# The last batch of a two-layer graph network: k pieces among its first steps, statistics a step later, one PSUM tile for each row block of the last projection

## The chip, the cores and the metric

The kernel runs on one core of a Trainium2 chip. The metric is the device time of one execution in microseconds; lower is better. The engines are named as the profile names them: PE (TensorE, matrix products into PSUM), DVE (VectorE), ACT (ScalarE), POOL (GpSimd, which works on SBUF only) and SP, whose queue issues most DMA transfers.

## The reference, cut to what matters

Two layers on x of shape 32 x 512 x 512 (batches, nodes, features), with one 512 x 512 graph `adj` for all batches.

```python
# layer 0
mi, mj = x @ Wi.T, x @ Wj.T
x = layernorm(x + deg * (mi + b) + adj @ mj)
# layer 1: masked attention, 8 heads of 64
q, k, v = split_heads(x @ Wq.T + bq), split_heads(x @ Wk.T + bk), split_heads(x @ Wv.T + bv)
attn = softmax(where(adj == 0, -inf, q k^T / 8))
x = layernorm(x + (attn v) @ Wo.T + bo)
```

All of it is float32. Each layer norm takes mean and variance over the 512 features of a row.

## The kernel before

**Pieces.** The 512 x 512 products with Wi, Wj, Wq, Wk, Wv and Wo are not done as 4 x 4 block products but by a seven-product scheme on 256 x 256 quarters. `piece(kind, b, i, bank)` issues one of the seven products (i from 1 to 7) of one projection (`l0` for layer 0, `q`, `k`, `v`, and `pj` for the output projection): four matrix instructions, or eight for `l0`, into a PSUM bank `mma` or `mmb`, then an evacuation on DVE (L445, L456, L465 or L472) or ACT (L434). Pieces of one group (X: 1, 2; Y: 6, 7, 4; Z: 5, 3) accumulate into the same bank, and each needs one weight tile, which SP loads ahead into a ring of seven. Combinations of quarters that the pieces need (`combos`, L396) are subtractions on POOL.

**Attention.** For a batch b there are eight steps: two groups g of four heads, four chunks kc of keys. A step does `scores` (L481, into two `sc` tiles of PSUM), exponentials in place on ACT (L485), a multiplication with the 0/1 graph on DVE (L486, result `e`, four buffers), and a step later `values` (L503) from e. `presum` adds up the e tiles of the chunks: the first two chunks on POOL (L492), later ones on DVE (L494). At the end of a group, `sums` (L513) makes the sums over keys on PE, `drain` (L518) copies them to SBUF on ACT, `invert` (L522) takes reciprocals in four parts on DVE, `scale` (L538) multiplies the values with them into `oT`, and `tell` (L526) adds up the reciprocals for a check that decides at the end of the program whether a slower general version must run.

**Order.** The order of instructions on each engine is the order in which the Python code issues them; there is no scheduler behind it. `PERIODS[n]` lists the work that is issued between the steps of batch n − 1's attention: layer 0 and the projections of the batch n, the output projection of the batch before last, the first parts of the batch after. `by_steps` spreads a period's list over its eight steps by cost (1.73 us a piece), with the halfway mark of the last ordinary period carried over to period 31. `phase_a(32)`, the end of period 31, holds five of the seven k pieces of the last batch, 31 (counted from 0). Period 32 is `last_steps`: beside the attention of batch 31 there are only the seven `pj` pieces of batch 30, its statistics (`stats`: L289, L290 on DVE, L291 to L293 on POOL), its scaling (`apply`, L296 on ACT), its `store`, and `last_part`. In each step the period's work comes after the scores and values; the `rest` of a finished group (inverts, scales, tell) and late presums are issued between the pieces, one after a piece, or in step 0 all of it at once after the first piece or `FLUSH`.

**The end.** `last_part` is batch 31's output projection without the seven-product scheme: per row block ic (four of 128 rows) an identity product that brings in the residual, and four products c with Wo, of which c = 2 and 3 need the oT of the second group of heads. `ACC[ic]` is the PSUM place of a row block: banks mma and mmb for blocks 0 and 1, and for blocks 2 and 3 the halves of one `sc` tile. `last_rows` takes a block's statistics, scales it on ACT and stores it. The final group of heads has no drain: `invert(1, ic, 0)` takes the reciprocals from the sums in PSUM, and `tell_all` makes both check sums on DVE (L533).

Of the kernel before, what the change touches and what calls it, by code (L numbers as in the profile page):

```python
# [14 lines left out]
OP = mybir.AluOpType  # L15
# [10 lines left out]
def gnn_attention_kernel(  # L26
# [36 lines left out]
    nc = tc.nc  # L63
    B, N, D = x.shape
# [15 lines left out]
    def work(shape, name, bufs, dtype=FT):  # L80
        return pools.work.tile(shape, dtype, name=name, bufs=bufs)
# [4 lines left out]
    def mm_tile(bank):  # L86
        return psum.tile([P, 512], FT, name="mm" + bank, bufs=1)
# [4 lines left out]
    def sc_tile():  # L92
        return psum.tile([P, 2, N], FT, name="sc", bufs=2)
# [36 lines left out]
    def load_w(t, src, eng):  # L130
        eng.dma_start(t, rows(src))
        return t
# [21 lines left out]
    for name, src in (("wv", wvT), ("wq", wqT)):  # L154
        t = load_w(work([P, NC, D], "v", 2), src, nc.sync)
# [31 lines left out]
    told = const.tile([P, B * 4 + 1], FT, name="told")  # L187
# [193 lines left out]
    def quarter(src, j, n):  # L381
        return src[:, 2 * j:2 * j + 2, Q * n:Q * n + Q]

    def ot_quarter(b):
        return lambda j, n: OT[b, j][:, :, Q * n:Q * n + Q]
# [89 lines left out]
    E, ES, PV, RL = {}, {}, {}, {}  # L475
# [30 lines left out]
    def sums(g, kcs=(1,), last=1):  # L506

        if g not in RL:
            RL[g] = (sc_tile()[:, 0, :], work([P, N], "rl", 1))
        for kc in kcs:  # L510
            for h in range(4):
                src = ES[h // 2] if kc == 1 else E[h // 2, kc]
                nc.tensor.matmul(RL[g][0][32 * h:32 * h + 32, :], ones[:, :32], src[:, h % 2, :], start=(kc == 1), stop=(kc == last))  # L513

    def drain(b, g):

        j = 2 * (b * 2 + g)
        nc.scalar.activation(RL[g][1], RL[g][0], AF.Identity, accum_out=told[:, j:j + 1])  # L518

    def invert(g, part, src=1):  # L520
        c = slice(part * P, (part + 1) * P)
        nc.vector.reciprocal(RL[g][1][:, c], RL[g][src][:, c])  # L522

    def tell(b, g):
        j = 2 * (b * 2 + g) + 1
        nc.vector.reduce_sum(told[:, j:j + 1], RL.pop(g)[1], axis=AX.X)  # L526

    def tell_all(b, g):

        pl, rl = RL.pop(g)  # L530
        j = 2 * (b * 2 + g)
        nc.gpsimd.memset(told[:, j + 1:j + 2], 0.0)
        nc.vector.tensor_tensor_reduce(pl, pl, rl, 1.0, 0.0, OP.add, OP.add, told[:, j:j + 1])  # L533

    def scale(b, g, r, c=slice(0, N)):
        if (b, g) not in OT:
            OT[b, g] = work([P, 2, N], "oT", 3)
        nc.vector.tensor_mul(OT[b, g][:, r, c], PV[g][r][:, c], RL[g][1][:, c])  # L538

    def rest(b, g):  # L540
        return [(invert, g, c) for c in range(4)] + [(scale, b, g, 0), (scale, b, g, 1), (tell, b, g)]
# [7 lines left out]
    FLUSH = (0.0, None)  # L549

    def z(f, *a):
        return (0.0, f, *a)

    def pc(kind, b, i, bank):
        return (2 * PC if kind == "l0" else PC, piece, kind, b, i, bank)

    ORDER = (1, 2, 6, 7, 4, 5, 3)

    LATE = (5, 3, 6, 7, 4)
    ALONE = ((1, "a"), (6, "b"), (2, "a"), (7, "b"), (5, "a"), (4, "b"), (3, "a"))  # L560

    def banks(n):

        return ("a", "b") if n % 2 == 0 else ("b", "a")

    def phase_a(n):

        A, K = banks(n)
        if n == B:
            return [pc("k", n - 1, i, bank) for i, bank in ((6, K), (5, A), (7, K), (3, A), (4, K))]  # L570
        xq, aq = lambda j, m: quarter(XD[n], j, m), lambda j, m: quarter(AX_T[n], j, m)
        g = [(GA, l0_gather, n, dc, A) for dc in range(DC)]
        k = [pc("k", n - 1, i, K) for i in LATE]
        res = []
        for i in range(DC):
            res += g[i:i + 1] + k[i:i + 1] + [z(l0_turn, n, i)]
            if i in (1, 2):
                res += [z(base, n, i - 1)]
            if n == 1 and i in (1, 3):
                res += [z(combine, "wo", nc.vector, i // 2)]  # L580
            if i == 1:
                res += [z(combos, TX, n, xq, (1,)), z(combos, TA, n, aq, (1,))]
        return res + [z(combos, TX, n, xq, (2,)), z(combos, TA, n, aq, (2,)),
                      z(combos, TX, n, xq, (3, 4)), z(combos, TA, n, aq, (3, 4)),
                      pc("l0", n, 1, A), k[4]]
# [111 lines left out]
    def last_steps():  # L697

        m = B - 2
        p = {i: pc("pj", m, i, bank) for i, bank in ALONE}  # L700
        c = [z(combos, TO, m, ot_quarter(m), (1, 2)), z(combos, TO, m, ot_quarter(m), (3, 4))]
        own = [(4 * GA, last_part, c, 0) for c in range(2)]
        return [[z(last_load), FLUSH, c[0], p[1], c[1]], [p[2], p[6]], [p[5], p[7], z(add_bo, B - 1, 0), z(add_bo, B - 1, 1)],
                [p[3], p[4], z(stats, m, 0), z(stats, m, 1)], [z(apply, m, 0), z(apply, m, 1), z(store, m)], [own[0]], [own[1]], []]

    def run(f):
        f[1](*f[2:])
# [2 lines left out]
    ACC = {}  # L710
# [5 lines left out]
    def last_part(c, half=None, ic=None):  # L716
        if c == 0:
            if half == 0:
                ACC[0], ACC[1] = mm_tile("a"), mm_tile("b")
            else:  # L720
                t = sc_tile()
                ACC[2], ACC[3] = t[:, 0, :], t[:, 1, :]
        for ic in (range(2 * half, 2 * half + 2) if ic is None else (ic,)):
            if c == 0:

                nc.tensor.matmul(ACC[ic], ident, XT[B - 1][:, ic, :], start=True, stop=False)
            nc.tensor.matmul(ACC[ic], OT[B - 1, c // 2][:, c % 2, ic * P:(ic + 1) * P], W["wo"][c // 2][:, c % 2, :],  # L727
                             start=False, stop=(c == 3))

    def last_rows(ic):  # L730
        y = XT[B - 1][:, ic, :]
        mv = work([P, 5], "mv", 12)
        ln_stats(mv, ACC[ic])
        nc.scalar.activation(y, ACC[ic], AF.Identity, bias=mv[:, 4:5], scale=mv[:, 3:4])
        nc.sync.dma_start(rows(out[B - 1])[:, ic, :], y)

    def flags():
# [5 lines left out]
        nc.vector.tensor_scalar(again, tot, -1.0, 1.0, op0=OP.mult, op1=OP.add)  # L743

    PERIODS = [first() + phase_c(0) + phase_a(1)]
    half = None
    for n in range(1, B):
        todo = phase_b(n) + phase_c(n) + phase_a(n + 1)
        if n < B - 1:
            half = sum(f[0] for f in todo) / 2  # L750

        PERIODS += [by_steps(todo, half)]
    PERIODS += [last_steps()]
    for f in PERIODS[0] + [f for p in PERIODS[1:] for todo in p for f in todo]:
        if f[1] is piece:
# [9 lines left out]
    for n in range(1, B + 1):  # L765
        b = n - 1
        extra = []
        for step in range(STEPS):
            g, kc = divmod(step, NC)
# [27 lines left out]
    sums(1, (1, 2), 3)  # L797
    values(B - 1, 1, 3)
    sums(1, (3,), 3)
    for c in range(2):  # L800
        last_part(c, 1)
    for ic in range(NC):
        c = slice(ic * P, (ic + 1) * P)
        invert(1, ic, 0)
        scale(B - 1, 1, 0, c)
        scale(B - 1, 1, 1, c)
        last_part(2, ic=ic)
        last_part(3, ic=ic)
        if ic > 0:
            last_rows(ic - 1)  # L810
    tell_all(B - 1, 1)
    last_rows(NC - 1)
    flags()
    fast.close()
    flag = nc.values_load(again[0:1, 0:1], min_val=0, max_val=1)
    with tc.If(flag > 0), tc.tile_pool(name="general", bufs=1) as pools.work:
# [26 lines left out]
        with tc.For_i(0, B, 1) as b:  # L843
            g = "general"
# [6 lines left out]
            for ic in range(NC):  # L851
                c = slice(ic * P, (ic + 1) * P)
# [10 lines left out]
            for ic in range(NC):  # L863
                c = slice(ic * P, (ic + 1) * P)
                nc.vector.tensor_copy(V[g][:, ic, :], product([(HT[g][:, dc, c], wv[:, dc, :]) for dc in range(DC)]))
            for hp in range(HP):
                c = slice(hp * P, (hp + 1) * P)
# [35 lines left out]
            for ic in range(NC):  # L903
                c = slice(ic * P, (ic + 1) * P)
# [45 lines left out]
```

## Time and profile before

| What | Value |
|---|---|
| median of 4 runs | 3703.95 us (3703.35 to 3707.35) |
| profiled execution | 3705.69 us |
| its span, first to last instruction | 3703.6 us |
| PE busy | 3667.4 us, 99% of the span |
| DVE, POOL, ACT busy | 65%, 52%, 28% |
| mean granted PE clock | 0.997 |
| PE busy in 3613 to 3656 us | 39.44 of 43 us |
| PE busy in 3656 to 3676 us | 17.30 of 20 us |
| PE busy in 3676 to 3704 us | 15.31 of 28 us |

The busy time of PE is the time in which a matrix instruction is under way. The last three rows are windows of the trace: the eight steps of the last batch's attention begin at 3615.58 us and its last sums at 3676.97 us; the last ACT instruction ends at 3697.50 us. The three windows show how much of PE's time is idle in the part of the program that the change touches.

### The profile page before, as it was taken

Reading aid. Unit: us, or ns where it says so; the run is one execution under the profiler, and the core shown is the slowest. Engines: PE = TensorE matmul, PEld = TensorE weight load, DVE = VectorE, ACT = ScalarE, POOL = GpSimd, SP = SyncE. Lnnn points to the kernel's source line nnn. Section 1 sums busy time; section 2 is a strip of 40 time slices with the busy share of each in tenths; the row PEclk is TensorE's granted clock in tenths of the full one; section 3 lists DMA queues with packets and bytes.
Section 4 is the critical chain, followed back from the end, with each engine's and each line's share of the span. In section 5 each row is a group of like instructions: output and inputs, shape, how many; then the busy total and the mean of one; then the engine's idle time right before and its main releaser. Section 6 shows DMA issues by size and latency. Waiting matters only on the chain.

```text
span 3703.6 us, 49651 instructions
## 1 busy us (share of the span) xinstructions
PE 3667.4 (99%) x18474; PEld 2512.4 (68%) x18474; DVE 2391.0 (65%) x3134; ACT 1028.7 (28%) x1482; POOL 1941.8 (52%) x1985
## 2 busy tenths in 40 slices
PE   8999999999999999999999999999999999999997
PEld 5666667666676767676767666666666676767663
DVE  4566666666666666666666666666666666666665
ACT  2222232323322222222232222232222322222322
POOL 3466445555455564455554555545555545555443
PEclk9999999999999999999999999999999999999999
DMA  8444555455554455554455544555544556455541
GB/s 252 121 125 136 150 153 160 120 142 140 156 159 137 131 136 150 157 152 127 136 144 156 160 134 132 138 148 160 149 131 133 148 151 163 126 136 140 151 137 47
DMA packets 797173, 530.02 MB, mean 143 GB/s; under 512 B 530432, under 2 KB 611840, under 8 KB 796928
## 3 DMA queue, kind: packets, MB, share of 16 engines
q1 hardware_dynamic: 780384, 494.78, 49.8%
q10 hardware_dynamic: 16320, 31.46, 2.3%
q8 instruction: 151, 2.47, 0.3%
q14 instruction: 94, 0.77, 0.1%
q0 software_dynamic: 224, 0.53, 0.0%
HBM read 453.25 MB, written 73.40 MB: 142 GB/s over the span
## 4 chain that ended last, share of the span: by engine, by line
PE 96%; DVE 1%; SPq 1%; POOL 1%; DMA 0%; issue 0%; ACT 0%; DVEq 0%; POOLq 0%; ACTq 0%
PE mma L427 31%; PE mmb L427 31%; PE sc L481 13%; PE ov L503 12%; PE mmb L325 3%; PE mma L325 3%; PE sc L513 2%; SPq L113 0%; DVE e L486 0%; DVE rl L522 0%; DMA wv<-e 0%; SPq L144 0%; DVE st L289 0%; DMA xa<-hd 0%; PE sc L727 0%
## 5 line engine op out<-in xcount | busy, mean ns | idle before, releaser
L485 ACT ACTIVATE sc<-sc 128x1024 f32<-128x1024 f32 x512 | 493.1, 1006 | 1550.4 <-PE sc L481 1544.1
L486 DVE TENSOR_TENSOR e<-sc,edge 128x1024 f32<-128x1024 f32 x512 | 602.1, 1217 | 205.2 <-ACT sc L485 173.3
L427 PE MATMUL mmb<-ring,big 128*128 128x256 f32 x3144 | 733.0, 382 | 0.0
L427 PE MATMUL mma<-ring,big 128*128 128x256 f32 x3112 | 724.4, 381 | 2.5 <-ACT p L434 1.4
L427 PEld LDWEIGHTS mmb<-ring,big 128*128 128x128 f32 x3144 | 593.0, 190 | 132.1 <-issue 27.6
L427 PEld LDWEIGHTS mma<-ring,big 128*128 128x128 f32 x3112 | 585.8, 190 | 133.3 <-issue 26.5
L396 POOL TENSOR_TENSOR big<-big 128x512 f32<-128x512 f32 x376 | 492.7, 1339 | 32.1 <-DVE big L373 10.9
L481 PE MATMUL sc<-q,k 64*128 64x512 f32 x2048 | 509.0, 615 | 0.0
L503 PE MATMUL ov<-e,v 128*32 128x512 f32 x4096 | 492.5, 598 | 4.9 <-DVE oT L538 4.9
L492 POOL TENSOR_TENSOR es<-e 128x1024 f32<-128x1024 f32 x128 | 301.1, 2365 | 352.3 <-DVE e L486 352.3
L427 PE MATMUL mma<-big,ring 128*128 128x256 f32 x1808 | 432.1, 382 | 3.2 <-DVE k L465 3.2
L427 PE MATMUL mmb<-big,ring 128*128 128x256 f32 x1776 | 422.8, 381 | 1.0 <-DVE v L456 1.0
L291 POOL TENSOR_SCALAR mv<-mv 128x1 f32<-128x1 f32 x256 | 50.0, 195 | 670.5 <-DVE mv L290 658.0
L427 PEld LDWEIGHTS mma<-big,ring 128*128 128x128 f32 x1808 | 341.5, 190 | 77.0 <-issue 26.0
L427 PEld LDWEIGHTS mmb<-big,ring 128*128 128x128 f32 x1776 | 334.3, 190 | 73.4 <-issue 26.0
L503 PEld LDWEIGHTS ov<-e,v 128*32 128x32 f32 x4096 | 106.9, 109 | 352.2 <-issue 320.8
L204 POOL TENSOR_TENSOR xlo<-xh,xhi 128x512 fp32r<-128x512 f32 x128 | 164.1, 1294 | 336.9 <-ACT xhi L203 336.8
L481 PEld LDWEIGHTS sc<-q,k 64*128 64x128 f32 x2048 | 176.0, 186 | 207.4 <-issue 205.1
L340 POOL TENSOR_TENSOR big<-big,deg_r 128x512 f32<-128x512 f32 x124 | 174.1, 1404 | 266.8 <-DVE big L339 266.8
L494 DVE TENSOR_TENSOR es<-es,e 128x1024 f32<-128x1024 f32 x250 | 304.3, 1218 | 0.0
L445 DVE TENSOR_TENSOR xh<-xh,mma 128x512 f32<-128x512 f32 x186 | 126.7, 681 | 266.3 <-PE mma L427 266.3
L445 DVE TENSOR_TENSOR xh<-xh,mmb 128x512 f32<-128x512 f32 x186 | 126.7, 681 | 263.2 <-PE mmb L427 263.2
(155 smaller groups left out, 3660.7 us busy)
## 6 DMA issues: line engine op xcount, KB each, us to landing
ring<-wo SPq DMA_DIRECT2D x217, 256.0 KB, 2.8
ring<-wq SPq DMA_DIRECT2D x160, 256.0 KB, 3.9
ring<-wv SPq DMA_DIRECT2D x160, 256.0 KB, 3.4
ring<-wk SPq DMA_DIRECT2D x160, 256.0 KB, 3.3
ring<-wi SPq DMA_DIRECT2D x155, 256.0 KB, 2.7
ring<-wj SPq DMA_DIRECT2D x155, 256.0 KB, 2.6
xh<-in_x_dram SPq DMA_DIRECT2D x32, 1024.0 KB, 5.5
xa<-in_x_dram SPq DMA_DIRECT2D x124, 256.0 KB, 4.0
```

The lines of the kernel that those rows point to most:

```text
L204: nc.gpsimd.tensor_sub(lo, xs, hi.bitcast(FT))
L325: nc.tensor.matmul(pm, parts[w][:, jc, :], adjR[:, jc, :], start=(w == 0 and jc == 0), stop=(w == 1 and jc == NC - 1))
L340: nc.gpsimd.tensor_tensor(XD[b][:, dc, :], XD[b][:, dc, :], deg_r, op=OP.mult)
L396: nc.gpsimd.tensor_tensor(dst, p, q, op=OP.subtract)
L427: nc.tensor.matmul(pm[:, c * Q:(c + 1) * Q], lhs, rhs, start=first, stop=(kc == 1 and n == len(terms) - 1), skip_group_check=True)
L445: nc.vector.tensor_tensor(d, d, pm, op=OP.add)
L481: nc.tensor.matmul(ps[:, s, :], KT[b, hp // 2][r, hp % 2, kc * P:(kc + 1) * P], QT[b, hp // 2][r, hp % 2, :], start=True, stop=True)
L485: nc.scalar.activation(ps, ps, AF.Exp, scale=QSCALE)
L486: nc.vector.tensor_tensor(e, ps, edge[:, kc:kc + 1, :].to_broadcast([P, 2, N]), op=OP.mult)
L492: nc.gpsimd.tensor_add(ES[i], E[i, 0], E[i, 1])
L494: nc.vector.tensor_add(ES[i], ES[i], E[i, kc])
L503: nc.tensor.matmul(PV[g][r][32 * h:32 * h + 32, :], V[b][:, kc, c0:c0 + 32], E[h // 2, kc][:, h % 2, :], start=(kc == 0), stop=(kc == NC - 1))
```

## The change

The first pieces of the list: two of batch 31's k pieces, 7 and 4, leave period 31 and go to the first step of period 32, around piece 1 of batch 30's output projection. The three that stay in period 31 come as 5, 6, 3 instead of 6, 5, 7, 3, 4. Piece 4 of batch 30's projection moves from step 3 to step 4, its statistics from step 3 to step 5, and its scaling and store from step 4 to step 6.

In the end, each of the row blocks 2 and 3 has an `sc` tile of its own. The final sums are drained by ACT like the others, reciprocals are taken from the copy, and `tell` and the drain's own sum replace `tell_all`. The early parts of row blocks 2 and 3 (identity, c = 0, c = 1) no longer come all before the late parts of block 0: block 2's come before block 0's late parts, block 3's before block 1's.

```diff
     if n == B:
-            return [pc("k", n - 1, i, bank) for i, bank in ((6, K), (5, A), (7, K), (3, A), (4, K))]
+            return [pc("k", n - 1, i, bank) for i, bank in ((5, A), (6, K), (3, A))]
...
     def last_steps():
         m = B - 2
-        p = {i: pc("pj", m, i, bank) for i, bank in ALONE}
+        A, K = banks(B)
+        p = {i: pc("pj", m, i, K if i in (6, 7, 4) else A) for i in ORDER}
         c = [z(combos, TO, m, ot_quarter(m), (1, 2)), z(combos, TO, m, ot_quarter(m), (3, 4))]
         own = [(4 * GA, last_part, c, 0) for c in range(2)]
-        return [[z(last_load), FLUSH, c[0], p[1], c[1]], [p[2], p[6]], [p[5], p[7], z(add_bo, B - 1, 0), z(add_bo, B - 1, 1)],
-                [p[3], p[4], z(stats, m, 0), z(stats, m, 1)], [z(apply, m, 0), z(apply, m, 1), z(store, m)], [own[0]], [own[1]], []]
+        k = [pc("k", B - 1, i, K) for i in (7, 4)]
+        return [[z(last_load), k[0], FLUSH, c[0], p[1], c[1], k[1]], [p[2], p[6]], [p[5], p[7], z(add_bo, B - 1, 0), z(add_bo, B - 1, 1)],
+                [p[3]], [p[4]], [own[0], z(stats, m, 0), z(stats, m, 1)], [own[1], z(apply, m, 0), z(apply, m, 1), z(store, m)], []]
...
     def last_part(c, half=None, ic=None):
         if c == 0:
             if half == 0:
                 ACC[0], ACC[1] = mm_tile("a"), mm_tile("b")
             else:
-                t = sc_tile()
-                ACC[2], ACC[3] = t[:, 0, :], t[:, 1, :]
+                ACC[ic] = sc_tile()[:, 0, :]
...
     sums(1, (3,), 3)
-    for c in range(2):
-        last_part(c, 1)
+    drain(B - 1, 1)
     for ic in range(NC):
         c = slice(ic * P, (ic + 1) * P)
-        invert(1, ic, 0)
+        invert(1, ic)
         scale(B - 1, 1, 0, c)
         scale(B - 1, 1, 1, c)
+        if ic < 2:
+            last_part(0, 1, ic + 2)
+            last_part(1, 1, ic + 2)
         last_part(2, ic=ic)
         last_part(3, ic=ic)
         if ic > 0:
             last_rows(ic - 1)
-    tell_all(B - 1, 1)
+    tell(B - 1, 1)
     last_rows(NC - 1)
```

The banks of the seven `pj` pieces stay the same (1, 2, 5, 3 in mma; 6, 7, 4 in mmb). `tell_all` and the argument `src` of `invert` are removed.

More of the change, by code (lines that the diff above doesn't have):

```diff
@@ L518, in drain, with invert @@
         nc.scalar.activation(RL[g][1], RL[g][0], AF.Identity, accum_out=told[:, j:j + 1])
-    def invert(g, part, src=1):
+    def invert(g, part):
         c = slice(part * P, (part + 1) * P)
-        nc.vector.reciprocal(RL[g][1][:, c], RL[g][src][:, c])
+        nc.vector.reciprocal(RL[g][1][:, c], RL[g][1][:, c])
     def tell(b, g):
@@ L526, in tell @@
         nc.vector.reduce_sum(told[:, j:j + 1], RL.pop(g)[1], axis=AX.X)
[L528 to L533, printed above, removed]
     def scale(b, g, r, c=slice(0, N)):
@@ L559, in gnn_attention_kernel @@
     LATE = (5, 3, 6, 7, 4)
-    ALONE = ((1, "a"), (6, "b"), (2, "a"), (7, "b"), (5, "a"), (4, "b"), (3, "a"))
     def banks(n):
```

## The prediction

> **What bounds the kernel now.** First the page, its chain of work that ended last:
>
> ```profile
> PE 96%; DVE 1%; SPq 1%; POOL 1%; DMA 0%; issue 0%; ACT 0%; DVEq 0%; POOLq 0%; ACTq 0%
> ```
>
> The kernel is TensorE (PE) work from end to end. The change keeps every matrix product, so it can only win or lose time in which PE waits, and in the stretch after the last sums, where PE is no longer the bound. So I read next the timeline from 3569 us on, for idle time ahead of PE's groups (in brackets: us, releaser):
>
> ```profile
> 3583.62 1.92 PE L503 MATMUL ov<-e,v 128*32 128x512 f32 x16 [0.64 <-DVE oT L538]
> ...
> 3602.78 1.99 PE L427 MATMUL mmb<-big,ring 128*128 128x256 f32 x8 [0.98 <-DVE v L456]
> ...
> 3625.30 1.92 PE L503 MATMUL ov<-e,v 128*32 128x512 f32 x16 [1.19 <-DVE oT L538]
> ...
> 3651.75 1.06 PE L513 MATMUL sc<-es,ones 128*32 128x512 f32 x8 [1.99 <-DVE e L486]
> ...
> 3658.70 1.92 PE L503 MATMUL ov<-e,v 128*32 128x512 f32 x16 [3.09 <-DVE oT L538]
> ...
> 3694.49 0.70 DVE L289 BATCH_NORM_STATS2 st<-sc 128x6 f32<-128x512 f32 x1 [1.47 <-ACT xh L734]
> ```
>
> Five PE waits of 7.9 us in all, and in the tail a statistic that waits for ScalarE (ACT). The chain of waits in order of time says what stands behind two of them:
>
> ```profile
> 3625.99 1.29 POOL big L396
> 3627.28 3.68 POOL xh L442 x3
> 3630.97 2.46 POOL big L396 x2
> 3633.42 4.63 POOL es L492 x2
> 3638.08 1.22 DVE e L486
> ...
> 3647.29 0.70 DVE st L289
> ...
> 3650.59 1.12 DVE e L486
> 3651.75 1.97 PE sc L513 x16
> ```
>
> From the last scaled oT of batch 30 the path runs through four kinds of POOL work to VectorE's (DVE's) e, which writes a buffer that the presum on POOL still reads; later the statistics (four L289/L290 pairs) stand ahead of e, and the sums on PE need that e to free their PSUM buffer.
>
> The profiled execution took 3705.69 us (span 3703.6, 2.09 around it), 1.74 above the median of 3703.95; the terms below are differences inside its span, and I subtract them from the median.
>
> **The change, part by part.** I lay the built order of the changed program's instructions over the durations of these rows: a piece 1.73 us (1.83 to 1.93 behind another tile shape), the scores of a step 1.92, its values 1.85, a sums group 0.86; sums to drain 1.10, drain to reciprocal 0.73, four reciprocals to the first oT 3.49, oT to values 0.74.
>
> *Two k pieces moved.* Batch 30's last four steps hold 3, 4, 4, 3 pieces instead of 4 each, and batch 31's first step three instead of one. Work on PE: nothing (−3.46 and +3.46); what counts is waits.
> - Step 5 of batch 30's period: the values wait for oT. Before, its last reciprocal stood behind a q evacuation that waited for the fourth piece; now it follows directly, so oT comes 1.15 us earlier (3581.73 for 3582.88), but PE arrives 1.73 earlier. The wait grows by 0.6.
> - The wait of 0.98 at 3602.78 (a bank whose evacuation stood late on DVE) goes. Before, two groups in bank mmb followed each other there, the second waiting for the first one's evacuation; now the first k piece there is 5, in mma, and the banks alternate. −1.0.
> - First step of batch 31: PE has 5.4 us of pieces instead of 1.9 between the sums and the scores. The oT chain is 1.8 us longer, because on DVE the evacuation of the first k piece (3.0 us after the sums start, 0.6 long) now stands ahead of the reciprocals. PE reaches the values at 8.25 us after the sums, oT is there at 7.9: the 1.19 goes, −1.2, with 0.4 to spare.
> - POOL's chain above starts 1.8 us later after the sums but PE's scores come 3.5 later, so the 0.26 that PE lost at step 3's scores (2.18 us for 1.92, 3638.23 to 3640.41) goes too: −0.25. What is late next: DVE's e of step 2 ends just as those scores need its buffer.
>
> *Pieces 3 and 4 of pj apart, statistics a step back.* Without the statistics ahead of e, step 4's sums find their buffer free: −2.0. But step 3 is one piece shorter, while DVE's run from e of step 2 to e of step 3 keeps its 5.64 us (3638.08 to 3643.72, with two L494 at 1.7 beside POOL's L378, where L494 else takes 1.22). Counted from the sums, e of step 3 frees its buffer at 27.5 and PE asks at 26.7: a new wait of 0.8 to 1.0, or none if the L494 run at 1.22. I take 0.9, as the rows beside L378 are the same rows.
> - Piece 4 now lies between step 4's sums and step 5's scores, in the wait of 3.09. It fills 1.7 us of it, but its evacuation stands on DVE ahead of the reciprocals and delays them by 1.7. Left: 3.0, −0.1.
> - Statistics in step 5: on POOL their twelve small operations (5.0 us, 3648.30 to 3653.32) now stand between the two presums L492. Queued behind: the second presum; who waits: the second e of step 6, which needs its buffer, then the scores of step 7, which need that e's PSUM. The second presum ends 10 us after the first starts; e comes 3.3 us late, step 7's scores 1.1. +1.1. Bounds: 0 (if POOL's operations ran with no gaps) to 3.3 (if nothing hid it).
> - apply and store of batch 30 move behind: 2.9 us of ACT between step 6's and step 7's exponentials, free there; the 1 MB store is issued some 24 us before the last row, and landed in 5.5 us or less in rows of its size. Nothing. The wo load's eight issues (3.7 us of SP) pass two ring loads that are used three steps later: nothing.
>
> *The tail, from the start of the last sums (3676.97).* Before, the last ACT starts 19.75 us later (3696.72). After: a drain on ACT comes between, so the first reciprocal is at 1.83 instead of 1.10. PE needs no oT until 0.97 + 0.96 + 2 x 0.86 = 3.65 (identity and two products of row block 2); oT is there at 3.3, so the 0.73 costs nothing. It costs up to 0.73 if oT came later than 3.65. Then two products for block 0 (end 5.37), three for block 3 (7.95), two for block 1 (9.67; block 1's end was at 9.7 before too), two for block 2 (11.4). DVE: statistics of block 1 at 9.87, reciprocal 10.7, oT 11.65, PE 11.99 to 14.0 for block 3; its statistics at 14.0, and from there 2.23 to the last ACT (3694.49 to 3696.72) is 16.25. Before, block 1's statistics stood behind block 2's scaling, 0.5 later; and as blocks 2 and 3 shared a tile, block 2's statistics waited for block 3's products (3691.45) and block 3's for block 2's ACT (3694.49), 3.0 more. −3.5. What follows (last DMA, end: 3697.50 to 3703.6) moves with it.
>
> Sum: +0.6 −1.0 −1.2 −0.25 −2.0 +0.9 −0.1 +1.1 −3.5 = −5.5 us, so 3698.5.
>
> PE's longest wait stays about 3 us, and the granted clock of these stretches is 1.00 up to 3694, through the 3.09; it falls to 0.50 only after the last products. The Trainium skill (TensorE: Matmul & The Clock Gate, Part 1: The HAM clock gate) says that an idle window of about 3.4 us halves the clock, and that the window runs freely. By that rule a wait of 3.0 stays just inside and the trace agrees so far; by it a wait stretched past 3.4 would cost what the fourth rival below says.
>
> **The rivals.**
> 1. The new waits are hidden: no wait for e in steps 4 and 7 and none added in batch 30's step 5. For: they hang on 0.3 to 1 us of DVE order and on the slow L494. Against: the rows of POOL's statistics are regular, 1.27 each. −5.5 −0.9 −1.1 −0.6 = −8.1: 3695.9.
> 2. Slower than before: POOL's run from oT to e of step 2 is the bound in batch 31's first steps, and now has no margin. If its 12.1 us (L396, L442, L492) stretch, each us is a us of PE. For: L378 ran at 1.73 beside L494, a plain row at 1.25, ratio 1.4. Against: in these rows it runs beside e and evacuations and keeps 1.25. At 1.4 it takes 4.9 more, 3703.4; above a ratio of 1.46 (5.6 us) the change is slower; at 1.6 it is 3705.8.
> 3. The middle gives nothing: waits only move on, and the tail alone counts. For: DVE is busy 31.3 of 43 us and takes each early PE back in the next step. −3.5 plus the step-5 and step-7 costs of 1.7: −1.8, 3702.1.
> 4. The clock: a wait of 3.0 grows past a window and halves the clock for a while. The windows view has lowered clocks of 0.85 and 0.54 between 54 and 60 us and of 0.67 and 0.71 between 105 and 116, so stretches of some 3.4 to 7 us. Cost half of that: 3700.2 to 3702.0. Against: 3.09 passed without it.
>
> **How the numbers follow.** A change of 0.2% is 7.4 us, about what a measurement of this kernel can tell from no change. Forecast: 0.56, between −7.5 and −3.4 by the bounds above (step 7 between 0 and 3.3, e between 0 and 1); a tenth of it lies past 7.4. Rival 1: 0.28, nearly all past 7.4. Rival 2: 0.06; slower by over 7.4 would need a ratio of 2.07, which is half of its chance at most. Rival 3: 0.06. Rival 4: 0.04. Faster by over 0.2%: 0.06 + 0.26 = 0.32; slower by over 0.2%: 0.03; within: 0.65. The range reaches from rival 1 with the tail 1 us better, 3694.9, almost to rival 3, 3701.5.
>
> **What would show it.** In the timeline after: no bracket at the values of batch 31's step 1 and at step 4's sums; about 3.0 ahead of step 5's values; a wait of 1 for e in step 7's scores, with a presum on POOL just before; 16.3 us from the last sums to the last ACT. Wrong if the tail keeps 19 us, if PE waits over 2 us for e in step 2 or 3 of batch 31 (rival 2), or if the granted clock is below 1.00 before the last products.

## The result, and the profile after

The changed kernel takes 3698.27 us (median; 3695.32 to 3701.78), the kernel before in the same comparison 3704.29 us (3700.61 to 3708.73). The ratio is 0.9983, 95% interval 0.9978 to 0.9987. The forecast was 3698.5 us. The profiled execution took 3699.72 us with a span of 3697.9.

All traces below are cut at the same five places: **A** from the scores of step 4 in batch 30's attention to batch 30's last sums, **B** from there to the values of batch 31's step 5, **C** to the last sums, **D** to the start of the last ACT instruction, **E** to the end of the span. A to D are differences of two start times in the timeline, E of the span and a start time. What lies ahead of A is not touched by any edit, but A begins anywhere between 3565.69 and 3569.94 us in the traces, and E wanders between 6.36 and 7.03; the time of a single execution carries both.

| us | A | B | C | D | E |
|---|---|---|---|---|---|
| before | 49.98 | 39.46 | 18.27 | 19.75 | 6.88 |
| after | 45.90 | 40.01 | 19.66 | 16.24 | 6.40 |
| difference | −4.08 | +0.55 | +1.39 | −3.51 | −0.48 |
| forecast | −3.86 | +0.81 | +1.1 | −3.5 | 0 |

(The forecast's row is its terms regrouped: two pieces of 1.73 leave A and enter B; beside them A holds +0.6 and −1.0, and B the terms from −1.2 to −0.1.) First the page's chain of work that ended last, after:

```profile
PE 96%; DVE 1%; SPq 1%; POOL 1%; DMA 0%; issue 0%; ACT 0%; POOLq 0%; DVEq 0%; ACTq 0%
```

The same as before: still TensorE from end to end. The timeline after, at the places that were shown of before, and two new ones (start, duration, engine, line, output and inputs; in brackets the idle time ahead and what ended it):

```profile
3582.95 1.92 PE L503 MATMUL ov<-e,v 128*32 128x512 f32 x16 [1.26 <-DVE oT L531]
...
3623.86 1.92 PE L503 MATMUL ov<-e,v 128*32 128x512 f32 x16
...
3643.04 2.26 PE L481 MATMUL sc<-q,k 64*128 64x512 f32 x8 [0.49 <-DVE e L486]
...
3646.97 1.04 PE L513 MATMUL sc<-es,ones 128*32 128x512 f32 x8
...
3655.60 3.22 PE L503 MATMUL ov<-e,v 128*32 128x512 f32 x16 [2.88 <-DVE oT L531]
...
3665.35 2.37 POOL L492 TENSOR_TENSOR es<-e 128x1024 f32<-128x1024 f32 x1
...
3667.75 1.23 DVE L486 TENSOR_TENSOR e<-sc,edge 128x1024 f32<-128x1024 f32 x1 [1.86 <-POOL es L492]
...
3689.28 0.70 DVE L289 BATCH_NORM_STATS2 st<-sc 128x6 f32<-128x512 f32 x1 [0.49 <-PE sc L721]
```

Line by line: batch 30's step 5 waits 0.62 longer. Step 1's values have no bracket (1.19 before), nor have step 4's sums (1.99 before). Step 4's scores have a new wait of 0.49. Step 5's values still wait 2.88. The second e of step 6 waits for the second presum on POOL. The last statistics wait for PE alone, 0.49, where they had stood 1.47 behind ACT.

One row is not what was forecast: the values at 3655.60 last 3.22 us instead of 1.92. The windows view says why (columns: stretch, length, busy time of PE, PEld, DVE, ACT and POOL, granted PE clock, DMA share, GB/s):

```profile
3653.00:3655.00 2.00, 0.00 (x0) 0.00 (x0) 1.97 (x4) 0.83 (x1) 0.00 (x0) 0.96 0.00 0
3655.00:3657.00 2.00, 1.40 (x8) 0.40 (x12) 2.00 (x4) 0.00 (x0) 0.00 (x0) 0.50 0.00 0
3657.00:3659.00 2.00, 2.00 (x13) 0.45 (x6) 2.00 (x3) 0.00 (x0) 1.06 (x1) 0.69 0.00 0
3659.00:3662.00 3.00, 3.00 (x8) 1.18 (x7) 2.87 (x7) 0.00 (x0) 2.57 (x6) 1.00 0.00 0
```

From 0.8 us before the end of the wait of 2.88 on, the clock is at half: (0.04 x 2 + 0.50 x 2 + 0.31 x 2) / 0.5 = 3.4 us of it. Before, the wait of 3.09 at the same place had 1.00 throughout:

```profile
3657.00:3659.00 2.00, 0.30 (x4) 0.16 (x8) 1.90 (x4) 2.00 (x3) 0.00 (x0) 1.00 0.40 152
3659.00:3661.00 2.00, 2.00 (x17) 0.55 (x10) 2.00 (x4) 0.06 (x1) 0.00 (x0) 1.00 1.00 372
```

So the fourth rival's clock did come, and a clock below 1.00 before the last products is one of the prediction's own signs of being wrong; still the sum holds. The experiments had to say why.

### The profile page after: what moved, and what is told of

The parts are those of the page before. It is cut to its first block, busy times and chain, and to the rows that moved or that the text cites. A ratio compares the mean times of both kernels' runs of the same rounds, so it can differ in the third digit from the quotient of the medians.

```text
span 3697.9 us, 49649 instructions
## 1 busy us (share of the span) xinstructions
PE 3668.2 (99%) x18474; PEld 2513.6 (68%) x18474; DVE 2390.6 (65%) x3133; ACT 1029.2 (28%) x1484; POOL 1938.7 (52%) x1984
## 4 chain that ended last, share of the span: by engine, by line
PE 96%; DVE 1%; SPq 1%; POOL 1%; DMA 0%; issue 0%; ACT 0%; POOLq 0%; DVEq 0%; ACTq 0%
PE mma L427 31%; PE mmb L427 31%; PE sc L481 13%; PE ov L503 13%; PE mmb L325 3%; PE mma L325 3%; PE sc L513 2%; SPq L113 0%; DVE rl L522 0%; DMA wv<-e 0%; DVE e L486 0%; SPq L144 0%; PE sc L721 0%; SPq L166 0%; POOL es L492 0%
## 5 line engine op out<-in xcount | busy, mean ns | idle before, releaser
L494 DVE TENSOR_TENSOR es<-es,e 128x1024 f32<-128x1024 f32 x250 | 304.2, 1217 | 0.0
```

The source lines that it names most:

```text
L494: nc.vector.tensor_add(ES[i], ES[i], E[i, kc])
```

## Experiments

Medians are of timed runs; a single time is one execution. The first three kernels were timed beside the kernel before at 3705.48.

**Each part alone**, on the kernel before. First the tail (`tail_only`):

```diff
-                t = sc_tile()
-                ACC[2], ACC[3] = t[:, 0, :], t[:, 1, :]
+                ACC[ic] = sc_tile()[:, 0, :]
...
-    for c in range(2):
-        last_part(c, 1)
+    drain(B - 1, 1)
...
+        if ic < 2:
+            last_part(0, 1, ic + 2)
+            last_part(1, 1, ic + 2)
...
-    tell_all(B - 1, 1)
+    tell(B - 1, 1)
```

> The kernel before with the change's last projection alone (a tile for each row block, the drain, blocks 2 and 3 interleaved). Forecast's account: the middle stays as before (values of step 5 wait about 3.1 us, sums of step 4 about 2.0), and from the start of the last sums to the start of the last ACT instruction 16.2 us instead of 19.75; in all -3.5 us, 3700.8. If the drain lay on the path (0.73), 17.0 and -2.8. If the middle gives everything and the tail nothing, 19.7 and no change.

Measured: 3701.9 us, ratio 0.9989 [0.9979, 0.9998]; A 49.97, B 39.46, C 21.16, D 16.24, E 6.90. D is the change's to the hundredth, −3.51. C is 2.89 longer, though no instruction of C differs from before: in this trace the clock fell behind the unchanged wait of 3.09, and for (0.11 x 2 + 0.50 x 6 + 0.10 x 2) / 0.5 = 6.8 us, as its windows show:

```profile
3654.00:3656.00 2.00, 0.00 (x0) 0.00 (x0) 1.90 (x3) 2.00 (x4) 0.00 (x0) 0.89 0.04 14
3656.00:3662.00 6.00, 5.60 (x19) 1.59 (x20) 3.80 (x5) 0.75 (x1) 3.25 (x2) 0.50 0.45 170
3662.00:3664.00 2.00, 2.00 (x6) 0.92 (x5) 0.00 (x0) 0.00 (x0) 1.41 (x1) 0.90 0.00 0
```

Then the k pieces (`k_only`):

```diff
-            return [pc("k", n - 1, i, bank) for i, bank in ((6, K), (5, A), (7, K), (3, A), (4, K))]
+            return [pc("k", n - 1, i, bank) for i, bank in ((5, A), (6, K), (3, A))]
...
+        k = [pc("k", B - 1, i, banks(B)[1]) for i in (7, 4)]
+        return [[z(last_load), k[0], FLUSH, c[0], p[1], c[1], k[1]], ...
```

> The kernel before with the two k pieces moved alone (phase_a with 5, 6, 3; pieces 7 and 4 in the first step of the last batch). Forecast's account: wait of 0.98 ahead of a piece in batch 30's step 6 gone, wait of 1.19 at the values of step 1 gone, wait at the values of batch 30's step 5 0.64 plus 0.6; sums of step 4 still wait 2.0 for e and the values of step 5 still 3.1; in all -1.9 to -2.2 us, 3702.2. If waits only move on within batch 31 (third rival), the sums of step 4 wait 3 to 4 us and the sum is about 0.

Measured: 3703.18 us, ratio 0.9993 [0.9984, 1.0003], which does not tell it from no change; A 45.90, B 41.18, C 18.26, D 19.76. A to D are 2.36 less than before. The wait of step 1's values is gone; that of step 4's sums stays, 1.77. The wait of 3.09 ahead of step 5's values is there, with the clock at 1.00.

Then the statistics (`stats_only`):

```diff
-                [p[3], p[4], z(stats, m, 0), z(stats, m, 1)], [z(apply, m, 0), z(apply, m, 1), z(store, m)], [own[0]], [own[1]], []]
+                [p[3]], [p[4]], [own[0], z(stats, m, 0), z(stats, m, 1)], [own[1], z(apply, m, 0), z(apply, m, 1), z(store, m)], []]
```

> The kernel before with piece 4 of the projection in step 4, the statistics in step 5, scaling and store in step 6, and nothing else of the change. Forecast's account: the 2.0 us at step 4's sums goes, 0.5 to 1.1 come at step 4's scores, 1.1 at step 7's scores, the wait of step 5's values stays near 3.0: in all about 0, between -1.1 and +0.3 us, 3704. First rival's account (the new waits are hidden): -2 us, 3702.

Measured: 3703.78 us, ratio 0.9995 [0.9986, 1.0005], again not told from no change; A 49.98, B 38.32, C 19.91, D 19.76. What B wins (−1.14) C gives back (+1.64). Its waits are 0.73 at step 4's scores, none at its sums, and 2.89 at step 5's values, with the clock at half behind it. The sum of A to D is +0.51, just outside the −1.1 to +0.3 that was expected.

In the traces A to D give −2.36 (k), +0.51 (statistics) and −3.51 (tail, without the clock's 2.89), together −5.36; the change has −5.65. The parts add up to 0.3 us. By the traces, what was won is the k pieces and the tail; of the three timed ratios only the tail's lies clear of 1.

**The shared tile put back** (`shared_tile`), on the changed kernel:

```diff
-                ACC[ic] = sc_tile()[:, 0, :]
+                if ic == 2:
+                    t = sc_tile()
+                    ACC[2], ACC[3] = t[:, 0, :], t[:, 1, :]
```

> The changed kernel with row blocks 2 and 3 in the two halves of one tile again (all else as changed). If the tile is what counts in the tail: block 2's statistics wait for block 3's products and block 3's for block 2's ACT, and from the last sums to the last ACT 19.1 us instead of 16.24 (+3.0). If the order of the early products is what counts, 16.3 to 17.

Measured: 3700.94 us; A 45.90, B 40.02, C 19.91, D 19.28. D is 3.04 longer than the changed kernel's. Its timeline at the last two row blocks:

```profile
3686.91 0.70 DVE L289 BATCH_NORM_STATS2 st<-sc 128x6 f32<-128x512 f32 x1 [1.88 <-PE sc L723]
...
3689.13 0.78 ACT L730 ACTIVATE xh<-sc,mv 128x512 f32<-128x512 f32 x1 [3.38 <-POOL mv L293]
...
3689.94 0.70 DVE L289 BATCH_NORM_STATS2 st<-sc 128x6 f32<-128x512 f32 x1 [1.55 <-ACT xh L730]
```

The last statistics stand behind ACT's reading of the other half of the tile, as before the change. So 3.04 of the tail's 3.51 is the tile alone; the prediction had 3.0 for it and 0.5 for the order of the row blocks. The other 0.47 was not tried by itself.

**The changed kernel again** (`after_again`), to see whether its clock falls each time:

> The changed kernel once more, for the granted clock behind the 2.9 us wait of step 5's values. If the clock falls by where a freely running window lies, the values of step 5 may now run at full clock (1.85 us to the next matmul instead of 3.15), and then step 7's scores wait about 1.1 us for e, which the first trace hid (0.1); from step 5's values to the last sums 19.4 in one case and 19.7 in the other. If the length of the wait alone decides, 3.15 again.

Measured: 3698.62 us; A 45.90, B 40.02, C 19.68, D 16.25. The clock fell again behind the wait of 2.88 (step 5's values 3.27 us to the next product).

**The reciprocals ahead of piece 4** (`flush4`). In step 4 the evacuation of `pj` piece 4 stands on DVE ahead of the reciprocals, and these wait for the piece's products. A `FLUSH` issues them first:

```diff
-                [p[3]], [p[4]], ...
+                [p[3]], [FLUSH, p[4]], ...
```

> The changed kernel with the reciprocals, scales and tell of step 4 issued ahead of piece 4, so that its evacuation no longer stands before them on DVE. By the forecast's account of the 3.0 left at step 5's values: the wait falls to 1.3 to 1.5 us, the granted clock stays 1.00 there, sums to values 6.1 instead of 7.8 from the second sums group; step 7's scores then wait 1.1 to 1.8 us for e, as POOL's statistics stand where they stood. In all -1.0 to -1.7. If the wait has another cause than that evacuation, it stays 2.9.

Measured: 3697.34 us; A 45.90, B 38.31, C 21.89, D 16.22. B wins 1.7 and C loses 2.2, so the 1.0 to 1.7 that was expected in all did not come: A to D are 0.5 longer. The timeline of this kernel:

```profile
3651.11 1.92 PE L503 MATMUL ov<-e,v 128*32 128x512 f32 x16 [1.18 <-DVE oT L531]
...
3663.83 2.36 DVE L486 TENSOR_TENSOR e<-sc,edge 128x1024 f32<-128x1024 f32 x2 [3.72 <-POOL es L492]
...
3665.11 2.00 PE L481 MATMUL sc<-q,k 64*128 64x512 f32 x4 [1.70 <-DVE e L486]
3667.05 2.69 PE L503 MATMUL ov<-e,v 128*32 128x512 f32 x16
```

The wait ahead of step 5's values is down to 1.18 and these run at 1.92. But step 7's scores now wait 1.70 for the e behind the presum on POOL: the wait that the prediction priced at 1.1 and that the trace after did not show. And the clock fell behind this shorter wait; the windows have it at 0.56 and 0.73, and at 1.00 in the stretch ahead:

```profile
3663.00:3665.00 2.00, 0.41 (x2) 0.00 (x0) 1.17 (x2) 1.01 (x1) 0.80 (x1) 1.00 0.77 292
3665.00:3667.00 2.00, 1.89 (x4) 0.43 (x4) 1.19 (x2) 0.00 (x0) 0.00 (x0) 0.56 0.63 232
3667.00:3670.00 3.00, 3.00 (x25) 0.76 (x26) 1.22 (x1) 1.01 (x1) 0.00 (x0) 0.73 0.00 0
```

**The statistics a step later still** (`stats_late`), behind the second presum:

```diff
-   [own[0], z(stats, m, 0), z(stats, m, 1)], [own[1], z(apply, m, 0), z(apply, m, 1), z(store, m)], []]
+   [own[0]], [own[1], z(stats, m, 0), z(stats, m, 1)], [z(apply, m, 0), z(apply, m, 1), z(store, m)]]
```

> The changed kernel with the statistics in step 6 and scaling and store in step 7, so that the two presums on POOL follow each other. By the forecast's account: no wait for e in step 6 on the second presum, step 7's scores do not wait; the wait of step 5's values stays 2.9. From step 5's values to the last sums 18.3 at full clock, 19.6 if the clock is halved behind the wait. If presums are not the cause, e of step 6 still waits for POOL and 19.4 to 19.7 stays.

Measured: 3695.47 us; A 45.90, B 40.02, C 18.27, D 16.23. C is that of before. But in this trace the clock stayed at 1.00 behind the same wait:

```profile
3652.18 1.92 PE L503 MATMUL ov<-e,v 128*32 128x512 f32 x16 [2.89 <-DVE oT L531]
```

So C had lost two things at once, the statistics and the half clock, and this run doesn't tell which of them was worth 1.4 us.

**The wait filled** (`fill`) tells them apart. The changed kernel gets two products that nothing reads, so that PE is busy in part of the wait:

```diff
-                [p[3]], [p[4]], ...
+                [p[3]], [p[4], z(fill)], ...
+    def fill():
+        pm = mm_tile("a")
+        for i in range(2):
+            nc.tensor.matmul(pm, ident, XT[B - 1][:, i, :], start=True, stop=True)
```

> The changed kernel with two products more, whose result nothing reads, at the end of batch 30's step 4, 1.7 us of TensorE's time, so that it waits 1.2 us instead of 2.9 ahead of step 5's values while these values start at the same time. Theory A (the half clock lies over the wait for e in step 7, which costs as much): step 5's values at full clock, 1.85 us to the next product instead of 3.15, then a wait of 1.0 to 1.3 us ahead of step 7's scores, and from the values to the last sums 19.4 us; the time stays within 0.5 us of the changed kernel's. Theory B (the half clock is what makes these 19.7): no wait in step 7 and 18.3 us, about 1.4 us less than the changed kernel.

Measured: 3696.95 us; A 45.89, B 40.02, C 19.64, D 16.24. Its timeline:

```profile
3652.80 1.92 PE L503 MATMUL ov<-e,v 128*32 128x512 f32 x16 [1.17 <-DVE oT L531]
...
3664.93 2.48 DVE L486 TENSOR_TENSOR e<-sc,edge 128x1024 f32<-128x1024 f32 x2 [3.13 <-POOL es L492]
...
3666.21 1.13 PE L481 MATMUL sc<-q,k 64*128 64x512 f32 x4 [1.11 <-DVE e L486]
```

Theory A holds: A to D are within 0.02 us of the changed kernel's. The values are back at 1.92, the wait in step 7 appears with 1.11, and C is 19.64 as with the half clock (19.66). The sum from step 5 to step 7 is set by DVE and POOL; the half clock made PE late for a buffer that was not free anyway. Of C's 1.39 the statistics in step 5 are the whole.

**The last rows a block later** (`rows_late`), on the changed kernel: the statistics of a row block are issued on DVE behind the scaling of the block after the next, instead of ahead of it.

```diff
-        if ic > 0:
-            last_rows(ic - 1)
+        if ic > 1:
+            last_rows(ic - 2)
+    last_rows(NC - 2)
```

> The changed kernel with the rows of the last projection one block later on DVE, so that block 3's reciprocal stands before block 1's statistics. By the forecast's chain of the tail (block 1's statistics at 9.87, reciprocal 10.7, oT 11.65, products to 14.0): block 3's products follow block 2's without a gap and end 0.6 to 0.7 earlier, 15.5 us from the last sums to the last ACT instead of 16.24. If the chain runs over something else (POOL, ACT or the drain), 16.2 stays.

Measured: 3696.98 us; A 45.90, B 40.03, C 19.68, D 15.52. D wins 0.72. In the trace after, block 3's reciprocal and oT stood on DVE behind the statistics of block 1, and PE waited for that oT (0.45); here no late part waits for oT.

**All three** (`best_all`): the edits of `flush4`, `stats_late` and `rows_late` together, timed beside the changed kernel on the same chip.

> The changed kernel with three more edits: a flush of the transposes ahead of the last product with p in batch 30's step 4, the last batch's statistics in step 6 with their application and store in step 7, and last_rows one block later. Theory A (the three gains are in different places and add up): from the last sums of batch 30 to the values of step 5 38.3 us instead of 40.0, from these to the last sums 18.3 instead of 19.7, the tail 15.5 instead of 16.2, together 3.8 us less than the changed kernel, about 3694.5 us, and the ratio to the kernel before about 0.9972; the wait ahead of step 5's values about 1.2 us and the granted clock 1.00 there. Theory B (the sums of step 7 are bound by VectorE's chain, so that what is won in step 4 is lost before step 7): from the values to the last sums about 20, only the tail and the statistics' part is left, 2.1 us less than the changed kernel, about 3696.2.

> The changed kernel as it is, on the same chip as the kernel with three more edits: about 3698.3 us, ratio 0.9983; the wait ahead of step 5's values 2.9 us. Theory A (the clock falls behind that wait by where a window of fixed length happens to lie): full or half clock from case to case, from the values to the last sums 19.4 to 19.7 either way, since VectorE's e of step 7 is late by 1.1 us where the products are not. Theory B (the fall alone makes these 19.7): 18.3 where the clock stays at 1.00.

Measured: `best_all` 3692.9 us (3691.37 to 3694.09), ratio to the kernel before 0.9969 [0.9957, 0.9982]; `after_timed` 3698.05 us (3694.67 to 3700.81), ratio 0.9982 [0.9973, 0.9991]. `best_all` has A 45.90, B 38.32, C 18.26, D 15.52, E 6.97; `after_timed` 45.90, 40.02, 19.69, 16.24, 6.36. Theory A of the first: all three gains are there, 3.85 us of A to D. `flush4` lost its gain to the presum's chain, and with the statistics out of that chain it keeps it:

```profile
3651.45 1.92 PE L503 MATMUL ov<-e,v 128*32 128x512 f32 x16 [1.18 <-DVE oT L531]
...
3662.62 1.99 PE L481 MATMUL sc<-q,k 64*128 64x512 f32 x8
```

No wait in step 7 any more. The medians differ by more, 5.15; the 1.3 beyond these stretches is less than the two intervals leave open, and no stretch shows it. `after_timed` fell to half clock once more, with C at 19.69; the first theory of its expectation agrees, and `fill` with full clock is the other half of it.

## Why the prediction was right, point by point

- **Batch 30's step 5** (+0.6): 1.26 for 0.64, +0.62. **The bank wait** (−1.0): gone, 0.98. With the two pieces that is −3.82 of A's −4.08. The other 0.26 lies around the same bank wait: from the start of the piece ahead of it to the scores behind it PE took 4.79 us before, and takes 3.54 for two pieces after.
- **Step 1's values** (−1.2): no bracket. It holds with the k pieces alone too.
- **Step 3's scores** (−0.25): 1.92 us from these to the values, for 2.18.
- **Step 4's sums** (−2.0): no bracket in the change and in `stats_only`; still 1.77 in `k_only`. The statistics were what they waited for.
- **Step 4's scores** (+0.9): a bracket of 0.49, and their row lasts 2.26 for 1.99, as its second half waits for the second e. Together some 0.76. e came when forecast (27.45 us behind the sums, forecast 27.5); PE came 0.3 later than the forecast's 26.7.
- **Step 5's values** (2.88 for a forecast 3.0): as forecast, but the step behind it failed. "3.09 passed without it" was taken as evidence that this wait keeps the clock. Ten traces have a wait of 2.88 to 3.09 there: the clock fell in seven, and stayed in three (before, `k_only`, `stats_late`). The trace before had a warning, too: the 0.85 and 0.54 that the fourth rival quotes stand behind a wait of 1.97 us, at 55.74, so over the whole trace a wait of 3.0 was not "just inside". The fourth rival deserved far more than 0.04 as a mechanism; what decides is told below.
- **Step 7** (+1.1): the wait of 1 that was to show did not show after, but C grew by 1.39, 0.29 more than forecast. `fill` uncovers it: 1.11 us, e behind POOL's second presum.
- The sum missed the half clock and still came out. Part of that is luck, for the prediction did not see that the two would overlap; but there is a reason: a delay of PE in step 5 costs nothing up to about the 1.1 us that it would wait in step 7. The half clock cost 1.29 us there (3.15 us from these values to the next product, for 1.86), and C is nearly the same with it and without (19.66 and 19.64).
- **The tail** (−3.5): −3.51, of which 3.04 is the tile. From the last sums to the last ACT 16.24 for a forecast 16.25.
- **Rival 2** (POOL's chain stretches): no. From the chain of waits after:

```profile
3624.05 1.28 POOL big L396
3625.33 3.69 POOL xh L442 x3
3629.01 2.44 POOL big L396 x2
3631.46 4.65 POOL es L492 x2
...
3636.13 1.22 DVE e L486
```

POOL's four rows make 12.06 us, as before; the ratio is 1.00. PE's scores of step 3 show no wait in front of them. The rival's price was read from a mean: its four L378 rows of 1.73 are two of 1.27 and two of 2.26 in the trace before. The slow ones start inside an L494 on DVE and end 1.1 us behind it, and each L494 starts inside a row of POOL and ends 1.1 us behind that, as if the two ran one after the other. **Rival 3**: no, the middle (A to C) gave −2.14. **Rival 1**: no, each of its three waits cost time, the last one under the half clock. **Rival 4**: its clock came, for 3.4 us, but not its price of 1.7 to 3.5 us: 1.29 at the values, of which C shows nothing. The prediction took 7.4 us as about what a measurement of this kernel can tell from no change; 6.0 us were told, with a ratio of 0.9978 to 0.9987.

**When the clock falls.** In each of the 13 traces the granted clock changes only on a grid of 3.413 us, to within 0.01 us. In the trace after it falls at 67.44, 108.40, 3654.84 and 3692.39 us, which is 12, 1039 and 11 times 3.4133 us from one to the next, and a lowered stretch that ends inside the program is one or two such windows long. So it matters how the grid cuts a wait. In the seven traces that fell, one window holds 2.12 to 2.88 us of the wait ahead of step 5's values, and the clock is at half from the end of that window on. In the three that did not, the fullest window holds 1.81, 1.82 and 1.99 us. A sharp limit is not shown: the 1.97 us in the trace before, and the 1.70 of `flush4`, each inside one window, did halve the clock. With a limit near 2.05 us, between the 1.99 and the 2.12, a wait of 2.88 reaches it for 2.19 of the 3.41 us over which the grid can lie, so in some 64% of executions; that is an estimate from these figures.

The Trainium skill (TensorE: Matmul & The Clock Gate, Part 1: The HAM clock gate) gives a free-running window of about 3.4 us, and halves the clock after an idle one. The lengths agree: 3.4 us of half clock in the change and in `flush4`, 6.8 in `tail_only`, and the grid, with the same wait with and without a fall, fits a window that runs freely. The condition does not: the clock fell behind waits of 2.88 and 1.70 us, shorter than a window. Here the measurement decides; no run varied the idle share alone.

## What to carry to other kernels

When a wait is removed, follow the chain of the other engines to the next buffer that it frees: here the statistics on POOL stood ahead of a presum two steps before the wait that they caused, and an edit that won 1.7 us ahead of it lost it there until they were moved. A PSUM tile shared by two row blocks ties the second one's statistics to the first one's reader; a tile each was worth 3.04 us. Whether a wait of about 3 us costs its clock cannot be read from one trace, as it depends on where the grid cuts it; count with it, and fill or shorten the wait where the steps behind it have no slack.

## What was not expected of the hardware

The granted clock fell behind waits of 2.88 to 3.09 us in seven of ten traces and not in three, and once behind a wait of 1.70. Twice the instructions ahead of the wait were the same and the outcome was not (before and `tail_only`; the change and `stats_late`). What differed was the place of a grid of 3.413 us, on which the clock changes, against the wait. None fell behind the 1.17 to 1.18 us ahead of step 5's values in three traces. One stretch of 3.4 us cost 1.2 to 1.5 us at these values (3.10 to 3.40 us for 1.86), one of 6.8 us cost 2.9 us of C in `tail_only`, and nothing of it remained where the next wait was for another engine.
